# Moving DVE work, the heads' planes and the keys' step in a two-layer graph kernel, with unread products at both ends

## The chip, the cores and the metric

The kernel runs on one core of a Trainium2 chip. The metric is the device time in microseconds (us) of one execution. The engines are PE (TensorE, products), DVE (VectorE), ACT (ScalarE), POOL (GpSimd) and SP (SyncE), which here only issues transfers.

## The reference

64 graphs of 256 nodes with 512 features each go through two layers. Each layer normalizes and clips its input, and adds an attention over the graph's edges to it. Shapes: x (64, 256, 512), float32; adj (64, 256, 256), boolean. In layer 0, `adj` is a mask of what is left out; in layer 1 it is a mask of what is kept.

```python
# layer 0: 8 heads of 64
h = maximum(layernorm(x), 0)
m = h @ map_w.T + map_b                                  # split into heads: sem
n = sem / maximum(norm(sem), 1e-8)
cos_adj = ((n @ n.T) * ~mask > 0.1)                      # cosines over a threshold
q, k = m @ q_w.T + q_b, m @ k_w.T + k_b
p = softmax(where(mask, -1e10, q @ k.T / 8)) * keep      # keep: row's first mask entry is not set
a = cos_adj * p
s = h @ gcn_map_w.T + gcn_map_b
x = x + relu((a @ s) @ gcn_W.T / (a.sum(-1) + 1))
# layer 1: 4 heads of 64
h = maximum(layernorm(x), 0)
q, k, v = h @ Wq, h @ Wk, h @ Wv
attn = softmax(where(mask, q @ k.T / 8, -big))
x = x + (attn @ v) @ Wo + bo
```

## The kernel before

The kernel is a pipeline over the graphs. The function `period(i)` holds the work of four graphs at once: `g` (graph i) finishes its layer 0, `nx` (i+1) goes through its projections, `b` (i-1) finishes its layer 1, and `n2` (i+2) is normalized. `closing()` does the last graph. The order on each engine is the order of the program. PSUM is a ring of eight banks. A projection is done with seven products of blocks instead of eight (`seven_products`), written as a generator: each `next(...)` issues some products on PE, then the additions that read them on DVE.

The parts that the change touches (cuts are marked with `# ...`; a line number such as L546 in a profile is that of the whole file):

```python
def seven_products(left, wt, bias, dst, name, tokens_first=False):
    # ... step 1: products "24" (u2, u4 on ACT)
    pz = bank(f"{name}_z", shape)                         # step 2
    product("z", pz, 0, a11)
    out(0, 0, pz, p2)                                     # DVE, e.g. kT <- p_k_z, u2p_k
    p53 = bank(...); product("53", p53[:, 0], 3, s1); product("53", p53[:, 1], 2, s4)
    p5 = biased(p53[:, 0], 1, 5)                          # u5 on ACT
    yield
    product("z", pz, 4, s2)                               # step 3
    nc.vector.tensor_add(u4, pz, p5)                      # DVE: uup
    out(0, 1, p53[:, 1], u4)
    yield
    product("z", pz, 5, s3)                               # step 4
    out(1, 1, pz, p5); out(1, 0, pz, p4)
    yield

def heads_sent(g, n, av):      # per half n, two planes of 16 bits: ACT copies, SP issues a transpose (DMA)
    for k in range(2):
        nc.scalar.copy(flat.rearrange(...), bits[:, k])
        nc.sync.dma_start_transpose(out=g.heads[...], in_=flat)

def heads_joined(g, n):        # ACT copies the two transposed planes of half n into g.sem
    for k in range(2):
        nc.scalar.copy(bits[:, k, c], g.heads[:, k, c])

def total(g, sm):              # ACT copies the sums of the rows out of PSUM (homes)
    nc.scalar.activation(g.sms, sm, AF.Copy, accum_out=chk[:, g.i, 0:1])

def sums_back(g):              # PE turns the sums (rt), DVE inverts them (r) and applies keep (rk)
    # ...

def heads_added(g, t):         # L542 ff.
    o = sb2.tile([P, H0, DH], F32, tag="xn", name=f"o{g.i}_{t}")
    nc.vector.scalar_tensor_tensor(o, g.sem[:, t, :]..., 0.0, g.rk[:, t, :, None]..., op0=ALU.max, op1=ALU.mult)
    nc.gpsimd.tensor_add(g.xs[:, t, :], g.xs[:, t, :], o...)

def edges(g, home=None):       # POOL makes the edges of a later graph, SP transposes them (mask)
    # ...

def divided(b):                # L646: layer 1's outputs by the sums of their rows
    nc.vector.tensor_mul(b.avs1, b.avs1, b.z)

def result(b, t):              # L651: output product p_o, then DVE adds it to xs
    # ...

def period(i):
    # ... scores, masks, projections m, s, q of nx, cosines of g
    for n in range(2):
        heads_sent(g, n, values(g, n))
    if b:
        nc.scalar.copy(b.avs1, values1(b))
    next(q)                                               # step 4 of q: p_q_z
    total(g, sums(g, lambda c: [g.d[c]], "sm"))
    for n in range(2):
        heads_joined(g, n)
    k = keys(nx)
    next(k)                                               # step 1
    if b:
        nc.scalar.activation(b.rz, b.rz, AF.Copy, accum_out=chk[:, b.i, 3:4])
    sums_back(g)
    heads_added(g, 0)
    # ...
    next(k)                                               # step 2
    heads_added(g, 1)
    if n2:
        edges(n2, g.homes)
    if b:
        divided(b)
    moments(g, f"1_{i}")                                  # DVE: st, mv, rs
    next(k)                                               # step 3
    deviations(g)                                         # ACT: root of rs; DVE: its reciprocal
    normalized(g, f"1_{i}")                               # DVE: xn, twice
    # ...
    if b:
        for t in range(NT):
            result(b, t)                                  # PE: p_o
    # ...
    g.h1T = turned(g, f"1_{i}", "wide")                   # PE: p_t <- xn; ACT: hT
    # ...
    next(k)                                               # step 4, then layer 1's projections of g
```

In the last graph's `closing()` the cosines of two of four pairs of heads stand ahead of the sums `se`, and the other two behind them; the copy of the sums `z` on ACT (`spent`, only for a check of ranges at the end) stands ahead of the reciprocals that read `z` on DVE.

Of the kernel before, what the change touches and what calls it, by code (L numbers as in the profile page):

```python
# [150 lines left out]
def fast_path(ctx, tc, a, w, chk, out):  # L151
# [4 lines left out]
    nc = tc.nc  # L156
# [49 lines left out]
    def normalized(g, tag):  # L206
        g.xn = []
        for t in range(NT):
            xn = sb2.tile([P, D], F32, tag="xn", name=f"xn{tag}_{t}")
            nc.vector.tensor_scalar(xn, g.xs[:, t, :], g.mv[:, t, 0:1], g.rs[:, t:t + 1],  # L210
                                    op0=ALU.subtract, op1=ALU.mult)
            g.xn.append(xn)
# [289 lines left out]
    def heads_joined(g, n):  # L502

        bits = g.sem.bitcast(U16).rearrange("p t (c f k) -> p k c t f", k=2, f=P)
        c = slice(2 * n, 2 * n + 2)
        for k in range(2):
            nc.scalar.copy(bits[:, k, c], g.heads[:, k, c])  # L507

    def sums(g, parts, name):

        sm = bank(f"{name}{g.i}", [P, S])
        for c in range(NKC):
            ps = parts(c)
            for j, part in enumerate(ps):
                for s in range(2):
                    n, k = divmod(2 * c + s, 4)
                    nc.tensor.matmul(sm[32 * k:32 * (k + 1), :], w.two[:, n, :], part[:, s, :],
                                     start=(n == 0 and j == 0), stop=(n == 1 and j == len(ps) - 1))
        return sm

    def total(g, sm):
        g.homes = both_homes(g.i)
        g.sms = g.homes[:, 0, :]
        nc.scalar.activation(g.sms, sm, AF.Copy, accum_out=chk[:, g.i, 0:1])
# [17 lines left out]
    def heads_added(g, t):  # L542
        o = sb2.tile([P, H0, DH], F32, tag="xn", name=f"o{g.i}_{t}")
        nc.vector.scalar_tensor_tensor(o, g.sem[:, t, :].rearrange("p (h d) -> p h d", d=DH), 0.0,  # L544
                                       g.rk[:, t, :, None].to_broadcast([P, H0, DH]), op0=ALU.max, op1=ALU.mult)
        nc.gpsimd.tensor_add(g.xs[:, t, :], g.xs[:, t, :], o.rearrange("p h d -> p (h d)"))  # L546

    def heads_back(g):
        for t in range(NT):
# [61 lines left out]
    def values1(b):  # L611
        av = bank(f"av1_{b.i}")
        for c in range(NIC):
            weighed(av, c, b.v, b.e1[c], 2 * c)
        return av
# [29 lines left out]
    def divided(b):  # L645
        nc.vector.tensor_mul(b.avs1, b.avs1, b.z)  # L646
# [7 lines left out]
    def period(i):  # L654
        g, nx = graphs[i], graphs[i + 1]
        b, n2 = graphs.get(i - 1), graphs.get(i + 2)

        def off_edges(*cs):
            for c in cs:
                masked(g.e[c], g.mask, edges=False)  # L660

        def halved_sums(*cs):
            for c in cs:
                g.d[c] = halves(g.e[c], f"0_{i}_{c}")


        if b:
            b.e1 = [exps(products(b.k1T, b.q1T, c, f"sc1_{b.i}_{c}"), f"1_{b.i}_{c}") for c in range(NIC)]
        for c in range(NKC):
            g.e[c] = exps(products(g.kT, g.qT, c, f"sc0_{i}_{c}"), f"0_{i}_{c}")  # L670
        if b:
            for c in range(NIC):
                masked(b.e1[c], b.mask, edges=True)
        m, s = mapped(nx), messages(nx)
        next(m)
        next(s)
        if n2:
            nc.scalar.activation(n2.rs, n2.rs, AF.Sqrt)

        off_edges(0, 1)  # L680
        halved_sums(1, 0)
        if b:
            b.d1 = [halves(b.e1[c], f"1_{b.i}_{c}") for c in range(NIC)]
        units(g)
        next(m)
        off_edges(2)
        if n2:
            nc.vector.reciprocal(n2.rs, n2.rs)
        halved_sums(2)
        next(m)  # L690
        next(s)
        next(m)

        for c in range(NKC):
            far_off(g, c, cosines(g, c))
            if c == 0:
                off_edges(3)
                halved(nx, lambda: halved_sums(3))
        for c in range(NKC):
            far_added(g, c, 0)  # L700
        squares(nx)
        if n2:
            shifts(n2, f"0_{n2.i}")
            scaled(n2, f"0_{n2.i}", 0)
        q = queries(nx)
        next(q)
        if n2:
            sent(n2, 0)
            scaled(n2, f"0_{n2.i}", 1)
        if b:  # L710
            sums1(b, lambda c: [b.d1[c]])
            own(b, "qk1")
            inverted(b)
        p_n = norms(nx)
        next(s)
        if n2:
            sent(n2, 1)
        if b:
            spread_inverses(b)
            summed_up(b)  # L720
        next(q)
        lengths(nx, p_n)
        for c in range(2):
            far_back(g, c)
            far_added(g, c, 1)
        next(s)
        next(q)
        for c in range(2, NKC):
            far_back(g, c)
            far_added(g, c, 1)  # L730
        next(s)

        g.avs = sb1.tile([P, NKC, S], F32, tag="wide", name=f"avs{i}")
        for n in range(2):
            heads_sent(g, n, values(g, n))
        if b:
            nc.scalar.copy(b.avs1, values1(b))
        next(q)
        total(g, sums(g, lambda c: [g.d[c]], "sm"))
        for n in range(2):  # L740
            heads_joined(g, n)
        k = keys(nx)
        next(k)
        if b:
            nc.scalar.activation(b.rz, b.rz, AF.Copy, accum_out=chk[:, b.i, 3:4])
        sums_back(g)
        heads_added(g, 0)
        if n2:
            joined(n2, f"0_{n2.i}")
            join(n2, 0)  # L750
        next(k)
        heads_added(g, 1)
        if n2:
            edges(n2, g.homes)
        if b:
            divided(b)
        moments(g, f"1_{i}")
        next(k)
        deviations(g)
        normalized(g, f"1_{i}")  # L760
        if i == 0:
            w.finish_seven(w.wqk1)
            w.finish_seven(w.wv1)
        nc.scalar.activation(nx.rn, nx.rn, AF.Sqrt)

        nc.scalar.activation(spare[:, 1:], spare[:, :1], AF.Exp)
        if b:
            for t in range(NT):
                result(b, t)
            nc.sync.dma_start(out=out_t[b.i], in_=b.xs)  # L770
        if i + 3 < B:
            graphs[i + 3] = load(i + 3)
        g.h1T = turned(g, f"1_{i}", "wide")
        if n2:
            join(n2, 1)
        j = queries_keys1(g)
        for t in range(NT):
            nc.gpsimd.tensor_add(g.xs[:, t, :], g.xs[:, t, :], w.bo_b)
        next(k)
        next(j)  # L780
        v = values_in(g)
        next(v)
        nc.vector.reciprocal(nx.rn, nx.rn)
        spread(nx)
        for step in (j, v, j, v, j, v):
            next(step)
        if n2:
            n2.left_h = left_factors(n2.hT, "sh", n2.i)
        if i + 3 < B:
            moments(graphs[i + 3], f"0_{i + 3}")  # L790
            below_zero(graphs[i + 3])

    def closing():
# [3 lines left out]
        for c in range(NKC):  # L797
            g.e[c] = exps(products(g.kT, g.qT, c, f"sc0_{g.i}_{c}"), f"0_{g.i}_{c}")
        units(g)
        co = [cosines(g, c) for c in range(2)]  # L800
        for c in range(NKC):
            masked(g.e[c], g.mask, edges=False)
        se = sums(g, lambda c: both(g.e[c]), "se")
        for c in range(2):
            far_off(g, c, co[c])
        first = sb1.tile([P, S], F32, tag="rn", name="first")
        nc.scalar.activation(first, se, AF.Copy, accum_out=chk[:, g.i, 0:1])
        for c in range(2, NKC):
            far_off(g, c, cosines(g, c))
        if b:  # L810
            b.e1 = [exps(products(b.k1T, b.q1T, c, f"sc1_{b.i}_{c}"), f"1_{b.i}_{c}") for c in range(NIC)]
        for c in range(NKC):
# [23 lines left out]
        if b:  # L836
            nc.scalar.copy(b.avs1, av)
        normalized(g, f"1_{g.i}")
        nc.scalar.activation(spare[:, 1:], spare[:, :1], AF.Exp)
        if b:  # L840
            inverted(b)
# [18 lines left out]
        for c in range(NIC):  # L860
            for j, part in enumerate(both(g.e1[c])):
                for s in range(2):
                    nc.tensor.matmul(z[s * DH:(s + 1) * DH, c, :], w.ones, part[:, s, :], start=(j == 0),
                                     stop=(j == NT - 1))
        spent = sb2.tile([P, NIC, S], F32, tag="xn", name="spent")
        nc.scalar.activation(spent, z, AF.Copy, accum_out=chk[:, g.i, 2:3])
        av = values1(g)
        own(g, "qT")
        for t in range(NT):
            q = slice(t * P, (t + 1) * P)  # L870
            nc.vector.reciprocal(g.z[:, :, q], z[:, :, q])
            nc.vector.tensor_mul(g.avs1[:, :, q], av[:, :, q], g.z[:, :, q])
        nc.scalar.activation(spent, g.z, AF.Copy, accum_out=chk[:, g.i, 3:4])
        if b:
            result(b, 1)
# [5 lines left out]
    def normal_input(g):  # L881
        g.hT = turned(g, f"0_{g.i}", "hT")
        g.left_h = left_factors(g.hT, "sh", g.i)

    with tc.manual_schedule():
        spare = small.tile([P, 2], F32, tag="spare", name="spare", bufs=1)
# [14 lines left out]
            normalized(graphs[n], f"0_{n}")  # L901

        g = graphs[0]
        normal(0)
        normal_input(g)
        edges(g)
# [346 lines left out]
```

## Time and profile before

| | |
|---|---|
| time, median of 3 (range) | 3678.06 us (3676.8 to 3678.59) |
| span of the profiled execution | 3673.2 us |
| PE, DVE, ACT, POOL busy | 98%, 73%, 59%, 61% |
| mean granted clock of PE | 0.998 |

The profile's page gives the busy time of each engine, the costliest groups of instructions, and the chain of work that ended last. A group's line has the source line, the engine, the operation, what it writes and reads, how often, its busy time and mean length, and behind the second bar the idle time of its engine just before it with what ended it. The list of waits names who waited for whom, in us in total, times, and the longest. The timeline has the instructions in order, merged where they repeat. Idle time of an engine counts only where PE, or the end of the program, waits for it in turn.

### The profile page before, as it was taken

What the parts mean: (1) busy time and instruction counts of PE and PEld (TensorE: products, weight loads), DVE (VectorE), ACT (ScalarE), POOL (GpSimd) and SP (SyncE); (2) the same over time, 40 slices, a digit from 0 to 9 for tenths busy, and PEclk for the clock granted to TensorE, in tenths of its full rate; (3) what the DMA queues carried; (4) which work ended last, traced back from release to release, by engine and by line L of the source; (5) the groups of instructions that cost most, each with busy time, mean ns of one, the idle gap of its engine ahead of it and who ended that gap; (6) DMA issues with size and microseconds to landing.
All of it is one profiled execution on the core that took longest, in us unless ns stands there. A gap on an engine that the chain in (4) does not pass through costs nothing.

```text
span 3673.2 us, 78457 instructions
## 1 busy us (share of the span) xinstructions
PE 3590.6 (98%) x29441; PEld 3082.7 (84%) x29441; DVE 2677.3 (73%) x5549; ACT 2164.6 (59%) x5174; POOL 2234.5 (61%) x2044
## 2 busy tenths in 40 slices
PE   8999999999999999999999999999999999999998
PEld 7888888888888888888888888888888888888886
DVE  7767767777677776776777767767777677777776
ACT  4556556666565656665666556555666565656553
POOL 4656666566566665665656656666566566665662
PEclk9999999999999999999999999999999999999999
DMA  4222222222222222222222222222222222222221
GB/s 123 52 67 55 59 67 57 62 57 62 69 55 57 63 61 63 55 60 69 55 60 59 61 67 55 59 67 57 61 57 62 69 55 58 63 59 65 55 54 39
DMA packets 496296, 224.68 MB, mean 61 GB/s; under 512 B 407436, under 2 KB 462248, under 8 KB 495912
## 3 DMA queue, kind: packets, MB, share of 16 engines
q1 hardware_dynamic: 495176, 219.03, 23.6%
q8 instruction: 236, 3.87, 0.5%
q14 instruction: 148, 1.21, 0.1%
q10 hardware_dynamic: 544, 0.52, 0.0%
q0 software_dynamic: 192, 0.04, 0.0%
HBM read 94.41 MB, written 34.34 MB: 35 GB/s over the span
## 4 chain that ended last, share of the span: by engine, by line
PE 86%; DVE 5%; ACT 4%; DMA 2%; issue 2%; POOL 0%; DVEq 0%; SPq 0%; POOLq 0%
PE sc L420 9%; PE av L447 9%; PE p_q L286 7%; PE p_m L286 6%; PE p_o L651 6%; PE p_qk L286 6%; PE p_s L281 6%; PE co L457 5%; PE p_s_z L281 5%; PE p_qk_z L286 5%; PE p_m_z L286 5%; PE p_q_z L286 5%; PE p_v L575 3%; ACT sem L507 3%; DVE o L544 3%; PE p_v_z L575 2%
## 5 line engine op out<-in xcount | busy, mean ns | idle before, releaser
L440 POOL TENSOR_TENSOR d<-e 128x512 f32<-128x512 f32 x376 | 586.4, 1585 | 299.0 <-DVE e L436 296.6
L476 POOL TENSOR_TENSOR d<-d,e 128x512 f32<-128x512 f32 x504 | 651.5, 1325 | 27.9 <-DVE e L481 27.9
L546 POOL TENSOR_TENSOR xs<-xs,o 128x512 f32<-128x512 f32 x126 | 183.7, 1458 | 529.1 <-DVE o L544 529.1
L427 ACT ACTIVATE e<-sc 128x512 f32<-128x512 f32 x768 | 383.3, 648 | 61.2 <-PE sc L420 61.2
L263 POOL TENSOR_TENSOR sh<-hT 128x256 f32<-128x256 f32 x128 | 94.1, 735 | 503.1 <-ACT hT L220 251.1
L436 DVE TENSOR_TENSOR e<-e,mask 128x1024 f32<-128x1024 f32 x256 | 365.3, 1447 | 0.5 <-ACT e L427 0.5
L470 DVE SCALAR_TENSOR_TENSOR e<-co,e 128x256 f32<-128x256 f32 (+1 forms) x1024 | 282.1, 345 | 35.8 <-ACT up L467 35.8
L499 ACT COPY avs<-av 128x512 uint16<-128x512 uint16 x252 | 135.3, 589 | 285.8 <-PE av L447 285.8
L651 PE MATMUL p_o<-wo,own 128*128 128x512 f32 x512 | 235.3, 602 | 50.0 <-DVE own L646 48.9
L467 ACT ACTIVATE up<-co,below 128x128 bf16<-128x128 f32 x512 | 160.3, 365 | 183.1 <-PE co L457 177.7
L447 PE MATMUL av<-e,sem 128*64 128x256 f32 x2048 | 235.6, 382 | 0.3 <-DVE e L481 0.3
L420 PE MATMUL sc<-qT,kT 64*128 64x256 f32 x2048 | 233.7, 376 | 0.0
L311 DVE TENSOR_TENSOR qT<-p_q_z,u5p_q 128x256 f32<-128x256 f32 x64 | 27.2, 425 | 279.6 <-PE p_q_z L286 279.6
L420 PEld LDWEIGHTS sc<-qT,kT 64*128 64x128 f32 x2048 | 220.6, 187 | 1.1 <-ACT hT L220 0.3
L651 PEld LDWEIGHTS p_o<-wo,own 128*128 128x128 f32 x512 | 91.9, 189 | 152.8 <-issue 108.8
L447 PEld LDWEIGHTS av<-e,sem 128*64 128x64 f32 x2048 | 141.2, 137 | 86.8 <-issue 20.9
L481 DVE SCALAR_TENSOR_TENSOR e<-far,e 128x256 f32<-128x256 bf16 x256 | 202.7, 830 | 1.6 <-DMA far<-up 1.5
L197 DVE BATCH_NORM_STATS2 st<-xs 128x6 f32<-128x512 f32 x256 | 173.9, 679 | 26.2 <-POOL xs L546 21.7
L457 PE MATMUL co<-nT 64*128 64x256 f32 (+1 forms) x2048 | 185.0, 330 | 0.0
L457 PEld LDWEIGHTS co<-nT 64*128 64x128 f32 x2048 | 161.3, 187 | 19.5 <-issue 0.4
L507 ACT COPY sem<-heads 128x512 uint16<-128x512 uint16 x252 | 169.5, 761 | 9.0 <-DMA heads<-avs 8.6
L251 ACT COPY hT<-turn 128x1024 uint16<-128x1024 uint16 x124 | 168.4, 1358 | 0.0
(249 smaller groups left out, 9537.6 us busy)
## 6 DMA issues: line engine op xcount, KB each, us to landing
xs<-in_x_dram SPq DMA_DIRECT2D x64, 512.0 KB
nT<-by_rn SPq DMA_DIRECT2D x128, 256.0 KB
out_dram<-xs SPq DMA_DIRECT2D x63, 512.0 KB
own<-by_rz SPq DMA_DIRECT2D x126, 128.0 KB
ad<-in_adj_dram SPq DMA_DIRECT2D x64, 64.0 KB
far<-up SPq DMA_TRANSPOSE x256
heads<-avs SPq DMA_TRANSPOSE x252
turn<-flat SPq DMA_TRANSPOSE x248
```

The source lines that it names most:

```text
L281: nc.tensor.matmul(region, src[:, c, :], wt[:, block, c, :], start=p not in opened, stop=True, skip_group_check=True)
L286: nc.tensor.matmul(region[:, f, :], wt[:, block, c, f * P:(f + 1) * P], src[:, c, :], start=p not in opened, stop=True, skip_group_check=True)
L420: nc.tensor.matmul(ps[s][:, j, :], rows[h, c, j * P:(j + 1) * P], cols[h, c, :], start=True, stop=True)
L427: nc.scalar.activation(e[:, s, :], p.rearrange("p j q -> p (j q)"), AF.Exp, scale=SCALE)
L436: nc.vector.tensor_mul(e, e, m)
L440: nc.gpsimd.tensor_add(d, e[:, :, :S], e[:, :, S:])
L447: nc.tensor.matmul(av[s * DH:(s + 1) * DH, n, :], vs[:, j, (h0 + s) * DH:(h0 + s + 1) * DH], q[:, s, j * S:(j + 1) * S], start=(j == 0), s ...
L457: nc.tensor.matmul(ps[s][:, j, j * P:], g.nT[h, c, j * P:(j + 1) * P], g.nT[h, c, j * P:], start=(j == 0), stop=True, skip_group_check=True)
L470: nc.vector.scalar_tensor_tensor(e, p.rearrange("p j q -> p (j q)")[:, lo:hi], THRESHOLD, e, op0=ALU.is_gt, op1=ALU.mult)
L476: nc.gpsimd.tensor_add(g.d[c], g.d[c], g.e[c][:, :, half * S:(half + 1) * S])
L507: nc.scalar.copy(bits[:, k, c], g.heads[:, k, c])
L651: nc.tensor.matmul(p, b.avs1[:, c, t * P:(t + 1) * P], w.wo1[:, c, :], start=(c == 0), stop=(c == NIC - 1))
```

## The change

In a period: the division of layer 1's outputs goes from behind `heads_added` to right behind the last step of q; the sums of rows go ahead of that step; the first half of the heads' planes is copied before the sums, the second half after; the two additions of `heads_added` go from POOL to DVE; the third step of the keys goes behind the normalization; the range check of `rz` goes a few places later. They are meant to let PE's output product and its turning of xn start without waiting for DVE.

At the ends: `kept_busy` issues products that nothing reads, to keep PE's clock up (14 before the first graph, 9 in the closing); the third pair of cosines in the closing goes ahead of the sums; the copy `spent` goes behind the reciprocals.

```diff
@@ sums split into sums and summed (same products, same order)
@@ heads_added
-        nc.gpsimd.tensor_add(g.xs[:, t, :], g.xs[:, t, :], o.rearrange("p h d -> p (h d)"))
+        nc.vector.tensor_add(g.xs[:, t, :], g.xs[:, t, :], o.rearrange("p h d -> p (h d)"))
@@ period
             nc.scalar.copy(b.avs1, values1(b))
+        heads_joined(g, 0)
+        total(g, sums(g, lambda c: [g.d[c]], "sm"))
         next(q)
-        total(g, sums(g, lambda c: [g.d[c]], "sm"))
-        for n in range(2):
-            heads_joined(g, n)
+        if b:
+            divided(b)
+        heads_joined(g, 1)
         k = keys(nx)
         next(k)
-        if b:
-            nc.scalar.activation(b.rz, b.rz, AF.Copy, accum_out=chk[:, b.i, 3:4])
         sums_back(g)
         heads_added(g, 0)
+        if b:
+            nc.scalar.activation(b.rz, b.rz, AF.Copy, accum_out=chk[:, b.i, 3:4])
 ...
         heads_added(g, 1)
         if n2:
             edges(n2, g.homes)
-        if b:
-            divided(b)
         moments(g, f"1_{i}")
-        next(k)
         deviations(g)
         normalized(g, f"1_{i}")
+        next(k)
@@ closing
-        co = [cosines(g, c) for c in range(2)]
+        co = [cosines(g, c) for c in range(3)]
 ...
-        for c in range(2):
+        for c in range(3):
             far_off(g, c, co[c])
 ...
-        for c in range(2, NKC):
-            far_off(g, c, cosines(g, c))
+        far_off(g, 3, cosines(g, 3))
 ...
         normalized(g, f"1_{g.i}")
+        kept_busy(9, "warm1")
 ...
-        spent = sb2.tile([P, NIC, S], F32, tag="xn", name="spent")
-        nc.scalar.activation(spent, z, AF.Copy, accum_out=chk[:, g.i, 2:3])
         av = values1(g)
 ...
+        spent = sb2.tile([P, NIC, S], F32, tag="xn", name="spent")
+        nc.scalar.activation(spent, z, AF.Copy, accum_out=chk[:, g.i, 2:3])
         nc.scalar.activation(spent, g.z, AF.Copy, accum_out=chk[:, g.i, 3:4])
@@ start
+    def kept_busy(n, name):
+        p = bank(name, [P, P])
+        for _ in range(n):
+            nc.tensor.matmul(p, w.ident, w.ident, start=True, stop=True)
 ...
         g = graphs[0]
+        kept_busy(14, "warm0")
         normal(0)
```

More of the change, by code (lines that the diff above doesn't have):

```diff
@@ L511, in sums, with summed @@
         sm = bank(f"{name}{g.i}", [P, S])
-        for c in range(NKC):
+        summed(sm, parts, range(NKC))
+        return sm
+    def summed(sm, parts, cs):
+        for c in cs:
             ps = parts(c)
@@ L518, in sums @@
                                      start=(n == 0 and j == 0), stop=(n == 1 and j == len(ps) - 1))
-        return sm
     def total(g, sm):
@@ L737, in period @@
             nc.scalar.copy(b.avs1, values1(b))
+        heads_joined(g, 0)
+        total(g, sums(g, lambda c: [g.d[c]], "sm"))
         next(q)
-        total(g, sums(g, lambda c: [g.d[c]], "sm"))
-        for n in range(2):
-            heads_joined(g, n)
+        if b:
+            divided(b)
+        heads_joined(g, 1)
         k = keys(nx)
         next(k)
+        sums_back(g)
+        heads_added(g, 0)
         if b:
             nc.scalar.activation(b.rz, b.rz, AF.Copy, accum_out=chk[:, b.i, 3:4])
-        sums_back(g)
-        heads_added(g, 0)
         if n2:
```

## The prediction

> **What bounds the kernel now.** I read the busy shares first, then the list of waits restricted to PE, then the timeline of one period, then the chain of waits of a longer one. The first lines say that PE has next to nothing left to lose, and where the little is:
>
> ```profile
> PE 3590.6 (98%) x29441; PEld 3082.7 (84%) x29441; DVE 2677.3 (73%) x5549; ACT 2164.6 (59%) x5174; POOL 2234.5 (61%) x2044
> ...
> L546 POOL TENSOR_TENSOR xs<-xs,o 128x512 f32<-128x512 f32 x126 | 183.7, 1458 | 529.1 <-DVE o L544 529.1
> ...
> PE p_o L651 <- DVE own L646: 48.9, 61, 1.1
> ```
>
> PE is busy 3590.6 of 3673.2 us, so all its idle time is 82.6 us, some 14 us of it before its first and after its last product. One wait repeats every period: the output product p_o waits for the division `own` (61 times, 48.9 us, at most 1.1 us). A period (start of one group of scores to the next, read off the 64 repeats of the scores in the chain) is 56.50 us in 35 of the 62 full periods; the other 27 are longer, by 13.2 us together. The 62 take 3516.1 us. The timeline of the typical period that runs from 213.4 to 269.9 us (columns: start, length, engine, line, operation; idle time before it in brackets):
>
> ```profile
> 250.18 0.38 PE L533 MATMUL rt<-ident,homes 128*128 128x128 f32 x2
> ...
> 250.89 0.36 DVE L540 TENSOR_SCALAR rk<-r,keep 128x8 f32<-128x8 f32 x2
> ...
> 251.46 0.69 DVE L544 SCALAR_TENSOR_TENSOR o<-sem,rk 128x512 f32<-128x512 f32 x1 [0.20 <-ACT sem L507]
> ...
> 252.07 0.42 DVE L311 TENSOR_TENSOR kT<-p_k_z,u2p_k 128x256 f32<-128x256 f32 x1
> 252.23 1.27 POOL L546 TENSOR_TENSOR xs<-xs,o 128x512 f32<-128x512 f32 x1 [7.61 <-DVE o L544]
> ...
> 252.40 1.65 DVE L544 SCALAR_TENSOR_TENSOR o<-sem,rk 128x512 f32<-128x512 f32 x1
> ...
> 253.08 1.06 PE L286 MATMUL p_k_z<-sm,wk 128*128 128x128 f32 x8
> 253.97 0.68 DVE L646 TENSOR_TENSOR own<-own 128x512 f32<-128x512 f32 x1
> ...
> 254.13 1.65 POOL L546 TENSOR_TENSOR xs<-xs,o 128x512 f32<-128x512 f32 x1 [0.63 <-DVE o L544]
> 254.57 0.68 DVE L197 BATCH_NORM_STATS2 st<-xs 128x6 f32<-128x512 f32 x1
> 254.80 3.67 PE L651 MATMUL p_o<-wo,own 128*128 128x512 f32 x8 [0.66 <-DVE own L646]
> ...
> 255.81 0.69 DVE L197 BATCH_NORM_STATS2 st<-xs 128x6 f32<-128x512 f32 x1 [0.34 <-POOL xs L546]
> ...
> 256.76 0.17 DVE L200 TENSOR_SCALAR rs<-mv 128x2 f32<-128x2 f32 x1
> ...
> 257.83 1.01 DVE L210 TENSOR_SCALAR xn<-xs,mv,rs 128x512 f32<-128x512 f32 x2
> ...
> 258.52 1.09 PE L219 MATMUL p_t<-ident,xn 128*128 128x128 f32 x8
> ```
>
> The reader should see three things. The second o takes 1.65 us where the first takes 0.69, and it ends 0.55 us after the POOL addition beside it. The division stands behind it, and p_o behind the division. And p_t starts 0.13 us after the first xn (257.83+0.56=258.39) ends, so it too is held by DVE.
>
> How late is PE? The products of p_k_z start (1.06-0.275)/7=0.112 us apart (a product is 275 ns), so p_o was due at 253.08+8x0.112=253.98 and came at 254.80: 0.82 late. Those of p_o start (3.67-0.59)/7=0.44 apart, so p_t was due at 254.80+3.52=258.32 and came at 258.52: 0.20 late. A typical period thus holds 1.02 us that better order could give; 62 of them 63 us, and with the 13.2 us of the longer ones 76 us, 2.1%. That is the ceiling inside the periods.
>
> **What the Trainium skill says.** "SBUF — State Buffer", section "SBUF: two separate sides": VectorE and GpSimd share a port pair under an exclusive lock, which an operation with two SBUF inputs takes against a GpSimd operation that reads SBUF; the loser blocks until the other ends. The 1.65 beside the 1.27 agrees. "GPSIMD Engine Reference", section "3.1 Elementwise — side-by-side cycle accounting": an addition of two tensors is 1.96 times slower on GpSimd at 2048 elements; here 1.27 against 0.68 for a two-input 128x512 on DVE (`own`), 1.87. "TensorE: Matmul & The Clock Gate", section "Part 1: The HAM clock gate": the clock halves after an idle window of about 3.4 us and comes back after about as much work. Here p_t near the end takes 1.94 us for 8 after an idle 2.48, against 1.09 warm, and the clock averages 0.83 from 80 to 100 us after PE's idle 4.44: less idle time was enough.
>
> **The change part by part.**
>
> *Division.* It moves from behind the second o to right behind the p_q_z additions, where DVE has stood idle (4.47 us before those additions, 2.44 before the reciprocal of rt). With the sums now ahead of p_q_z, those additions end about 1.07 us later, near 249.2; the division then ends near 249.9, and rt comes at 250.18. Its inputs (the copy of av at 33.48 us into the period, z loaded by 31) are there. Cost on the path: 0. p_o no longer waits for it.
>
> *Additions.* Two POOL additions of 1.27 (one stretched to 1.65) become two of 0.68 on DVE. DVE's chain in the new order, with starts spaced as in the lines above, from o at 251.29 (rk ends at 251.25; the four copies of the heads' planes now end about 0.75 earlier, since two of them precede the sums' copy): addition +0.74 = 252.03, kT +0.61 = 252.64, o +0.33 = 252.97, addition +0.74 = 253.71, st +0.61 = 254.32, mv +0.72, st +0.10, mv +0.73, rs +0.22 = 256.09, the root on ACT +0.20, its reciprocal +0.24, xn +0.19 = 256.72, end 257.28, so p_t may start at 257.41 instead of 258.52. POOL's port is free then, so no 1.65.
>
> *The keys' step after the normalization.* It takes uup and kT out from between rs and its reciprocal, which were 0.88 us apart (256.76 to 257.64) and need 0.44 for ACT's root alone: 0.44 of the chain's gain is theirs. Their p_k_z is used after p_t, at 258.4; uup ends near 258.05, so nothing new waits.
>
> *What PE then does.* kT ends at 253.06, so the third p_k_z starts at 253.11 (+0.03). p_o follows at 254.01, p_t is due at 254.01+3.52=257.53 and ready at 257.41. It came at 258.52: gain 0.99, less 0.02 where my spacings are coarse: 0.97 x 62 = 60 us.
>
> *The longer periods.* Their transposes of the heads land up to 1.3 us later than a typical period can hide (the last landing 36.3 us into a typical period, up to 38.35 in the longest); in nearly all of these a 16 KB packet of the instruction queue (236 of them in the page's queue list) runs among the transposes. The chain of such a period, 1517.7 to 1574.8:
>
> ```profile
> 1551.61 3.95 DMA heads<-avs
> ...
> 1555.59 0.78 ACT sem L507
> ...
> 1557.00 0.41 DVE kT L311
> ```
>
> Here the new order is worse: kT now stands behind o and the first addition, and p_k_z waits for kT. I rebuilt each of the 62 periods from its landings with the spacings above: the 27 longer ones pay 0.2 to 1.3 us at p_k_z. The sum over all 62 is -57 us, so 3 us are given back.
>
> *The closing's third cosines, ahead of the sums.* The last transposes of far leave about 1.4 us earlier; PE then has the next scores (0.8 earlier) and the av products without the 0.28 wait and the stretched first group: about -1.1 us.
>
> *Unread products.* Nine at the end fill most of the 2.48 idle: p_t is warm, but its reader on ACT is held by a table load until 3641.7 anyway; what is left is p_qk at 1.95 instead of 2.77: -0.8. Fourteen at the start (28 passes, 0.24 each cold) end about when p_t is due at 8.25; the path there is the load of wq (lands at 15.26) and the DVE differences behind it: 0. *The spent copy later*: DVE's reciprocal starts 0.75 earlier, but p_o behind it is then limited by PE: 0. The first period, without a division, gains about 0.5 from the shorter chain.
>
> Sum: -57-0.5-1.1-0.8 = -59 us, 3619. I take 3621, because p_t and its second half each have only 0.12 us of slack in my rebuild.
>
> **The rivals.** (1) The DVE chain takes over as the bound: 0.12 us of slack is less than my spacings are sure of; each 0.1 us beyond it costs 6 us, so a chain 0.4 longer would give 3638. For it: p_t is held by DVE already. Against: the 1.65 and the POOL wait before st go for certain. (2) The transposes' landing becomes the bound more often, since kT waits for the additions: if half the periods lost 0.8, 3632. For it: the 27 long periods. Against: the copies on ACT are 0.75 earlier, so only landings later than 37.05 count. (3) Masks leave about 7 us earlier (POOL is free) and share the DMA engines with the heads' last transposes: a landing delayed by 0.6 in each period would give 3640. Against: they are issued behind them. (4) All of it hidden, long periods too: 3598.
>
> **Range and chances.** 3621, 8 in 10 between 3606 and 3639. Faster by over 2% needs under 3604.5, nearly the whole ceiling: 0.06. Slower by over 2% would need a new wait of over 2 us a period, which no line suggests: 0.01. Within 2%: 0.93.
>
> **What would show it.** Right: the wait of p_o on `own` gone, o at 0.69 both times, typical periods near 55.5, p_k_z waiting for kT a few tenths in periods with late heads, half-speed clock gone near 3640. Wrong: p_t waiting for xn in most periods (rival 1), ACT's copies of heads waiting in most (2, 3), or typical periods near 56.

## The result, and the profile after

| | before | changed |
|---|---|---|
| median (range) | 3677.43 us (3673.48 to 3678.59) | 3595.49 us (3594.11 to 3597.51) |
| ratio, 95% interval | | 0.9779 (0.9763 to 0.9796) |
| span of the profiled execution | 3673.2 us | 3595.7 us |
| start to second group of scores | 99.66 us | 101.05 us |
| typical period, x 62 | 56.50, 3503.0 us | 55.11, 3416.8 us |
| what the longer periods add to 62 typical ones | 13.1 us | 22.5 us |
| from the last period's end to the end | 57.42 us | 55.36 us |

The kernel is 2.2% faster: 82 us by the medians, 77.5 us between the two profiles, where I had predicted 56. The page of the changed kernel, first its busy times, then p_o's group (behind the second bar the idle time before it):

```profile
PE 3560.4 (99%) x29487; PEld 3057.2 (85%) x29487; DVE 2703.4 (75%) x5675; ACT 2169.1 (60%) x5174; POOL 2050.1 (57%) x1918
...
L654 PE MATMUL p_o<-wo,own 128*128 128x512 f32 x512 | 230.5, 593 | 0.0
```

The wait of p_o is gone altogether. PE's busy time also fell, by 30 us, although 46 products were added: something became cheaper on PE itself. The list of PE's waits over the full periods has one of size left:

```profile
PE p_k_z L286 <- DVE kT L311: 14.7, 21, 1.2
```

These 21 waits are in the longer periods. Before, this wait came to 1.4 us in 4 of them. The same stretch of the same period as in the prediction, which now runs from 212.8 to 267.9 us (start, length, engine, line, operation):

```profile
245.55 1.07 PE L521 MATMUL sm<-d,two 128*32 128x256 f32 x16
...
246.55 1.16 PE L286 MATMUL p_q_z<-sm,wq 128*128 128x128 f32 x8
...
247.55 1.95 PE L286 MATMUL p_k<-mT,wk 128*128 128x128 f32 x16
...
248.42 0.68 DVE L649 TENSOR_TENSOR own<-own 128x512 f32<-128x512 f32 x1
...
249.33 0.38 PE L536 MATMUL rt<-ident,homes 128*128 128x128 f32 x2
...
250.38 0.69 DVE L547 SCALAR_TENSOR_TENSOR o<-sem,rk 128x512 f32<-128x512 f32 x1
...
251.11 0.69 DVE L549 TENSOR_TENSOR xs<-xs,o 128x512 f32<-128x512 f32 x1
251.72 0.42 DVE L311 TENSOR_TENSOR kT<-p_k_z,u2p_k 128x256 f32<-128x256 f32 x1
252.05 0.68 DVE L547 SCALAR_TENSOR_TENSOR o<-sem,rk 128x512 f32<-128x512 f32 x1
252.23 1.12 PE L286 MATMUL p_k_z<-sm,wk 128*128 128x128 f32 x8
252.77 0.69 DVE L549 TENSOR_TENSOR xs<-xs,o 128x512 f32<-128x512 f32 x1
253.19 3.60 PE L654 MATMUL p_o<-wo,own 128*128 128x512 f32 x8
...
255.75 1.00 DVE L210 TENSOR_SCALAR xn<-xs,mv,rs 128x512 f32<-128x512 f32 x2
256.62 1.04 PE L219 MATMUL p_t<-ident,xn 128*128 128x128 f32 x8
```

The division stands in DVE's idle time, 0.68 us and off the path. From o to xn DVE takes 255.75-250.38=5.37 us, so p_t could start at 255.75+0.55+0.13=256.43 and starts at 256.62. That is 0.19 of slack: p_t no longer waits. What DVE still costs a typical period is 0.06 at the third p_k_z, which comes just behind kT (1.12 long here, 1.06 elsewhere). Set side by side, start to start, only six of PE's groups differ from before in a typical period:

| group (to the next one's start) | before | changed |
|---|---|---|
| p_q_z, last step of q | 1.088 | 0.995 |
| p_k, first step | 1.889 | 1.786 |
| p_k_z, third step, to p_o | 1.719 | 0.953 |
| p_o to p_t | 3.723 | 3.436 |
| p_t | 0.923 | 0.873 |
| last p_v to the scores | 0.653 | 0.564 |

These sum to 1.39 us. The third to fifth rows, 1.10, are the waits that I meant. The other 0.29 I had not in the sum at all. The sums and their neighbours in the kernel before (timeline of PE):

```profile
246.20 1.16 PE L286 MATMUL p_q_z<-sm,wq 128*128 128x128 f32 x8
247.29 1.07 PE L517 MATMUL sm<-d,two 128*32 128x256 f32 x16
248.29 2.05 PE L286 MATMUL p_k<-mT,wk 128*128 128x128 f32 x16
```

p_k has 16 products in both, and took 2.05 us here against 1.95 above, with no wait named in either. p_q_z is 1.16 long in both, but here the sums start 1.09 after it, and above p_k starts 1.00 after it. `128*32` says that the sums' weights are 32 columns wide; the products of q and k are 128 wide.

### The profile page after: what moved, and what is told of

The parts are those of the page before. It is cut to its first block, busy times and chain, and to the rows that moved or that the text cites. A ratio compares the mean times of both kernels' runs of the same rounds, so it can differ in the third digit from the quotient of the medians.

```text
span 3595.7 us, 78427 instructions
## 1 busy us (share of the span) xinstructions
PE 3560.4 (99%) x29487; PEld 3057.2 (85%) x29487; DVE 2703.4 (75%) x5675; ACT 2169.1 (60%) x5174; POOL 2050.1 (57%) x1918
## 4 chain that ended last, share of the span: by engine, by line
PE 93%; DMA 3%; DVE 1%; ACT 1%; issue 1%; SPq 0%; POOL 0%; DVEq 0%; POOLq 0%; ACTq 0%
PE sc L420 10%; PE av L447 8%; PE p_m L286 7%; PE p_q L286 7%; PE p_qk L286 6%; PE p_o L654 6%; PE p_s L281 6%; PE co L457 5%; PE p_qk_z L286 5%; PE p_m_z L286 5%; PE p_s_z L281 5%; PE p_k_z L286 5%; PE p_k L286 4%; PE p_q_z L286 4%; PE p_v L578 3%; PE p_v_z L578 2%
## 5 line engine op out<-in xcount | busy, mean ns | idle before, releaser
L507 ACT COPY sem<-heads 128x512 uint16<-128x512 uint16 x252 | 185.4, 767 | 69.2 <-DMA heads<-avs 67.9
L420 PEld LDWEIGHTS sc<-qT,kT 64*128 64x128 f32 x2048 | 198.5, 187 | 22.7 <-ACT hT L220 0.3
L781 POOL TENSOR_TENSOR xs<-xs,bo_b 128x512 f32<-128x512 f32 x126 | 157.8, 1274 | 0.0
```

Of the source, the lines that this page charges most:

```text
L420: nc.tensor.matmul(ps[s][:, j, :], rows[h, c, j * P:(j + 1) * P], cols[h, c, :], start=True, stop=True)
```

## The experiments

Each starts from the changed kernel unless said otherwise. "Typical" is the median of the 62 periods in its profile. For the changed kernel it stands for 55.11, the length of 29 of its 62 and the median when it ran again; the median of its first profile is 55.14. The ratio is against the kernel before on the same chip.

**Sums behind.** What is the unexplained 0.2 us?

```diff
         heads_joined(g, 0)
-        total(g, sums(g, lambda c: [g.d[c]], "sm"))
         next(q)
         if b:
             divided(b)
+        total(g, sums(g, lambda c: [g.d[c]], "sm"))
```

> The changed kernel with only the sums of rows put back behind the last step of q on PE (everything else as changed). Theory A, that PE pays for each switch between narrow (32-column) weights and full ones, and that the sums' new place next to the av products saves one pair of switches: the group p_q_z takes 1.09 instead of 1.00 us and the following p_k 1.89 instead of 1.79, the typical period goes from 55.11 to 55.31, the time from 3595 to about 3607. Rival B, that the PE gain of 0.2 us is slack of some other engine: typical period stays 55.11, time 3595.

Measured: 3604.58 us, ratio 0.9811 (0.9794 to 0.9827), typical 55.32. p_q_z went back to 1.088 and p_k to 1.888, and nothing else moved. A holds, B falls: the gain is PE's own, and lies at the borders, where one group of products ends and the next begins. Not only 32 columns do this: in the kernel before, a group also goes on 0.09 longer where 64 columns follow (p_s_z in front of av, 0.96 against 0.87) or 64 rows (p_m_z in front of the cosines, 0.98 against 0.89). Where only the moving side changes, from 128 to 256 columns, it costs nothing (p_m_z in front of p_s, 0.89). So the shape of the weights matters here, not the length of the products.

**Sums split.** The same cost doubled, with the same number of products.

```diff
-        total(g, sums(g, lambda c: [g.d[c]], "sm"))
+        sm = bank(f"sm{i}", [P, S])
+        summed(sm, lambda c: [g.d[c]], (0, 1))
         next(q)
+        summed(sm, lambda c: [g.d[c]], (2, 3))
+        total(g, sm)
```

> The changed kernel with the sums cut in two: half of them in front of the last step of q, half behind it. This adds two borders between narrow and full weights to the one that the changed kernel has there, with the same products. Theory A, that PE pays about 0.1 us at each border: typical period 0.2 above 55.11, the same as with all sums behind (55.31), time about 3605 to 3607. Rival B, that the sums' place matters through the products' number or through ACT's copy: typical period 55.1 to 55.15.

Measured: 3605.40 us, ratio 0.9815 (0.9800 to 0.9830), typical 55.44, 0.33 above. The timeline of PE in a period of it:

```profile
1912.72 0.64 PE L521 MATMUL sm<-d,two 128*32 128x256 f32 x8
1913.29 1.16 PE L286 MATMUL p_q_z<-sm,wq 128*128 128x128 f32 x8
1914.38 0.64 PE L521 MATMUL sm<-d,two 128*32 128x256 f32 x8
1914.95 2.05 PE L286 MATMUL p_k<-mT,wk 128*128 128x128 f32 x16
```

p_q_z and p_k pay the 0.09 and 0.10 again (1.09 from start to start; 2.05 long), and the two half sums take 0.57 each where the whole took 1.00. A holds, with 0.14 more in the period than it said, which is what the sums cost more as two groups than as one.

**Narrow groups together**, on top of the trial version below: zb goes behind the cosines, p_n ahead of the av products.

```diff
         squares(nx)
+        if b:
+            sums1(b, lambda c: [b.d1[c]])
 ...
-            sums1(b, lambda c: [b.d1[c]])
 ...
-        p_n = norms(nx)
 ...
-        lengths(nx, p_n)
 ...
+        p_n = norms(nx)
         g.avs = ...
 ...
             nc.scalar.copy(b.avs1, values1(b))
+        lengths(nx, p_n)
```

> The trial version before with two more groups of narrow weights moved next to others: zb behind the cosines, p_n in front of the av products. Theory A, that each pair of switches between narrow and full weights costs PE 0.2 us: typical period 0.1 to 0.3 below 55.11, time 6 to 18 us below that of the trial version it builds on. Rival B, that the 0.2 us of the sums' move was special to its place: typical period 55.1, no difference.

Measured: 3608.86 us, ratio 0.9822 (0.9806 to 0.9839), typical 55.49, 26 us slower than the version it builds on. Start to start, p_q fell by 0.09 and p_s_z by 0.10, but zb rose by 0.11 and p_n by 0.02: 0.06 less in all. I had miscounted the borders. There are four as before, since zb now stands between the cosines and p_q, and p_n between p_s_z and av. And PE now comes earlier to a product that DVE holds (its list of waits):

```profile
PE p_s_z L281 <- DVE uup_s L331: 14.2, 62, 0.5
```

With this wait p_s_z starts 0.39 later, and its restart takes 0.10 more, so the period grew by 0.44 over the trial version's 55.05. A's price of 0.1 at a border stands, its forecast does not.

**Division alone**, on the kernel before: `divided(b)` goes from in front of `moments` to behind `next(q)`, nothing else.

> The kernel before with only the division moved to behind the last step of q. Theory A, that the division on DVE alone held p_o, and xn then holds p_t: the wait of p_o is gone, the DVE chain ends 0.6 us earlier, p_t waits about 0.4 us, typical period near 55.9 instead of 56.50, time about 3640. Rival B, that the wait only moves from p_o to p_t: period 56.4 or more, time over 3670. Rival C, that the division alone gives all that the DVE moves give: typical period 55.4, time about 3610.

Measured: 3646.82 us, ratio 0.9926 (0.9909 to 0.9942), typical 56.13. A, less 0.2: p_o's wait is gone and p_t waits 0.58 us in the median period.

**Division back**, the reverse: `divided(b)` behind `heads_added(g, 1)` again.

> The changed kernel with only the division back behind the second addition on DVE. Theory A: p_o starts at 41.4 instead of 40.4 us into the period, typical period 56.1 to 56.2, time 3655 to 3662. Rival B, that the additions on DVE and the keys' new place had already made room for it: typical period 55.3 or less, time under 3610.

Measured: 3662.57 us, ratio 0.9967 (0.9956 to 0.9979), typical 56.21: A, at its upper edge. Its list of PE's waits shows the old wait with nearly the old total:

```profile
PE p_o L654 <- DVE own L649: 52.5, 61, 0.9
```

Without the division's move, all the others together give 11 of the 82 us.

**Additions back on POOL.**

```diff
-        nc.vector.tensor_add(g.xs[:, t, :], ...)
+        nc.gpsimd.tensor_add(g.xs[:, t, :], ...)
```

> The changed kernel with the two additions of heads_added back on POOL. Theory A, that the additions' move is a main part of the gain (as my prediction's chain had it): p_t waits 0.5 us or more for xn in a typical period, period 55.6 or more, time 3625 or more. Theory B, that the division's and the keys' new places do it all, because POOL's 1.27 can overlap with kT on DVE: xn at most 0.2 us later than now, inside PE's slack of 0.19, typical period 55.1 to 55.2, and kT ahead of the late heads' additions takes some tenths off the longer periods: time 3588 to 3600.

Measured: 3602.32 us, ratio 0.9804 (0.9788 to 0.9820), typical 55.28. Nearer to B, but 2 us outside it. A period's timeline (it starts at 2489.64):

```profile
2527.25 0.69 DVE L547 SCALAR_TENSOR_TENSOR o<-sem,rk 128x512 f32<-128x512 f32 x1
...
2527.86 0.42 DVE L311 TENSOR_TENSOR kT<-p_k_z,u2p_k 128x256 f32<-128x256 f32 x1
...
2528.02 1.28 POOL L549 TENSOR_TENSOR xs<-xs,o 128x512 f32<-128x512 f32 x1 [7.17 <-DVE o L547]
2528.19 1.66 DVE L547 SCALAR_TENSOR_TENSOR o<-sem,rk 128x512 f32<-128x512 f32 x1
...
2531.23 0.70 DVE L197 BATCH_NORM_STATS2 st<-xs 128x6 f32<-128x512 f32 x1 [0.56 <-POOL xs L549]
...
2532.82 1.00 DVE L210 TENSOR_SCALAR xn<-xs,mv,rs 128x512 f32<-128x512 f32 x2
2533.51 1.08 PE L219 MATMUL p_t<-ident,xn 128*128 128x128 f32 x8
```

The lock is back (1.66 beside 1.28), and still xn starts 43.18 us into the period, against 42.98 with the additions on DVE: POOL's first addition ran beside kT and the second o, and only its second one holds DVE (0.56 before the second st). So p_o to p_t takes 0.08 and p_t 0.05 more, the third p_k_z 0.06 less, as kT no longer stands behind an addition on DVE, and 0.09 more goes at the scores. The latter has no engine's work behind it that the profile shows: with the additions on POOL, before and here, the first scores product carries waits for both DVE and PE, with them on DVE only for DVE. That goes together in all the runs here (0.65 in the four with POOL, 0.56 in the ten with DVE); that the second wait is the cause is not shown.

**Keys' step back** in front of `deviations`.

> The changed kernel with only the third step of the keys back in front of the root and the normalization. Theory A, that its two additions on DVE lengthen the chain to xn by 0.44 us, of which PE's slack of 0.19 hides a part, and that a restart of PE after a wait costs up to 0.1 more: p_t waits, typical period 55.4 to 55.5, time 3612 to 3618. Rival B, that ACT's root hides them: 55.1, 3595.

Measured: 3611.93 us, ratio 0.9831 (0.9815 to 0.9848), typical 55.41: A. p_t starts 0.25 later, and pays 0.05 more once started.

**Sums alone**, on the kernel before: `total(...)` goes ahead of `next(q)`.

> The kernel before with only the sums in front of the last step of q. Theory A, that in the kernel before PE's 0.2 us are not what counts, because p_o waits for DVE: the copies of the heads on ACT and the rows' sums come earlier, o starts up to 0.43 earlier, and the period falls by that, to about 56.1, time about 3652. Rival B, that PE's 0.2 us come through alone: 56.3, about 3662. Rival C, that nothing comes through: 56.5, 3674.

Measured: 3658.21 us, ratio 0.9957 (0.9942 to 0.9972), typical 56.18, and 56.07 or 56.08 in 28 of the 62 periods. A in the typical period; the time is 6 us above what it named, with more and longer periods over it. Here the sums work through DVE's earlier start, not through PE's borders: o and the division start 0.38 us earlier in the period, p_o still waits for the division 61 times, and so starts 0.37 earlier.

**No unread products**: both calls of `kept_busy` out.

> The changed kernel without any unread products. Theory A, that the 14 at the start backfire (PE warms early, cools again while it waits for the differences of wm, and POOL's factors start earlier and block those differences on the shared port): the first scores start at about 44.4 instead of 45.2 us, and the end grows by about 0.8 us, so that the total stays within 1 us of 3595. Rival B, that the 14 at the start help: the first scores start later than 45.2. Side question: if the extra bank that they take in the ring is what took a wait off the first scores of a period, the typical period goes from 55.11 to 55.20 and the time to about 3601.

Measured: 3595.05 us, ratio 0.9783 (0.9767 to 0.9799), typical 55.11 with every group as in the changed kernel. The first scores start at 44.27 instead of 45.17, and the end takes 57.30 instead of 55.36 us: A at the start, and twice its loss at the end. In all there is no difference: the unread products gained nothing. The mean clock (before the DMA share and rate at the line's end) in one stretch of the start, first in the changed kernel, then in "sums behind", which has the 14 products too:

```profile
12.60:16.10 3.50, 3.10 (x14) 3.14 (x15) 2.10 (x4) 1.02 (x4) 2.48 (x4) 0.51 1.10 350
```

```profile
12.60:16.10 3.50, 3.21 (x29) 3.24 (x30) 2.07 (x4) 1.94 (x7) 2.37 (x4) 1.00 1.10 347
```

The 14 products warm the clock early, and PE then idles 2.33 us for the differences of wm. In the changed kernel the clock halves after that; in "sums behind", after 2.13 us idle, it doesn't, and the first scores start at 44.07. The section "Part 1: The HAM clock gate" of the Trainium skill's "TensorE: Matmul & The Clock Gate" has the clock judged in windows that run on by themselves; that one idle stretch costs the clock in one program and a like one does not in another agrees with it. The other runs say the same: of the seven profiles with the 14 products, four have a half-speed stretch there and first scores at 45.17 to 45.74, three have none and first scores at 44.03 to 44.25. Two of them, one of each kind, idled 1.91 us ("division back" and "keys' step back"). Without the 14, six of seven have first scores at 44.03 to 44.41, and one at 45.21, where the clock rose 4 us later than in the others. So the length of the idle time does not decide it, and the 0.9 us are in part chance.

**The longer periods: kT between o and the first addition** (the trial version; it also drops the 14 products, puts 12 into the first period's idle stretch, and makes layer 1's weight differences earlier there).

```diff
-        heads_added(g, 0)
 ...
-        next(k)
+        heads_added(g, 0, lambda: next(k))      # o, then kT, then the addition
         heads_added(g, 1)
```

What it is for shows in a longer period of the changed kernel (1209.4 to 1265.9):

```profile
1247.58 0.77 ACT L507 COPY sem<-heads 128x512 uint16<-128x512 uint16 x1 [2.37 <-DMA heads<-avs]
...
1248.38 0.69 DVE L547 SCALAR_TENSOR_TENSOR o<-sem,rk 128x512 f32<-128x512 f32 x1 [1.34 <-ACT sem L507]
...
1249.72 0.42 DVE L311 TENSOR_TENSOR kT<-p_k_z,u2p_k 128x256 f32<-128x256 f32 x1
...
1250.19 0.60 PE L286 MATMUL p_k_z<-sm,wk 128*128 128x128 f32 x3 [1.16 <-DVE kT L311]
```

The last heads land late, o waits for their copy, kT waits behind o and the addition, and PE behind kT. The last heads land 38.16 us into this period, 36.35 into a usual one. The queue list from 1241 to 1250 us has one packet of the instruction queue among 2471 of the transposes' queue:

```profile
q8 instruction: 1, 0.02, 1.1%
```

> A trial version on top of the changed kernel: the additions of the keys' second step (kT) go between o and the first addition, so that PE's third p_k_z need not wait behind the additions when the heads land late; no unread products at the start, but 12 in the first period's idle stretch; the differences of layer 1's weights earlier in the first period. Theory A, that kT behind the late heads is what the longer periods pay: PE's waits before p_k_z mostly go, but xn is late in those periods as well, so only 0.1 to 0.2 us of each is saved; the sum over the median period falls from 20.9 to 16 to 18 us, the start by 3 us; time 3586 to 3592. Rival B, that the wait of p_k_z is all there is: 1.0 us less in the worst periods, the sum falls to 8, time about 3579.

Measured: 3582.69 us, ratio 0.9752 (0.9736 to 0.9768), typical 55.05. Its PE waits:

```profile
PE p_t L219 <- DVE xn L210: 2.9, 12, 0.3
PE p_k_z L286 <- DVE kT L311: 0.4, 1, 0.4
```

The longer periods add 11.7 us to 62 typical ones instead of 22.5 (20.9 over the median, as A counts), more of a gain than A said and less than B: p_k_z's wait is all but gone, and a smaller one of p_t for xn took its place. Two gains were not expected: 0.06 in the typical period, as p_k_z no longer waits for kT at all (0.953 fell to 0.893), and 4.4 us instead of 3 at the start.

**Both once more on one chip.**

> The changed kernel once more, to stand on one chip beside the trial version: 3592 to 3598, typical period 55.11; the time that the longer periods add (15 to 23 us over the median period so far) is chance, from where the instruction fetches fall.

> The trial version with kT between o and the first addition once more: 3579 to 3585, typical period 55.05, 10 to 14 us below the changed kernel on the same chip, of which some 4 are at the start, 4 in the typical periods and the rest in the longer ones.

Measured: changed 3594.13 us (3590.92 to 3596.21), ratio 0.9781 (0.9767 to 0.9794); trial 3583.44 (3582.03 to 3584.61), ratio 0.9753 (0.9739 to 0.9766). The ranges do not meet: the trial version is 10.7 us faster than the changed kernel. Its longer periods add 15.5 us this time, against 18.9, a gain of 3.4 instead of the 9 to 11 above. How much it gains there is thus not settled, and A is the nearer this time. Between these two profiles the start gives 4.8 us, the typical periods 3.8, and the end 0.6.

## Why the prediction was wrong, point by point

The direction and the wait were right, the size was not: 3595.5 lies below the range, whose lower end was 3606.

- *"That is the ceiling inside the periods"*: this is the step that failed. I measured how late p_o and p_t came and took the rest of PE's sequence as fixed. It is not. Against my 0.97 per typical period stand 1.39: 0.196 at the sums' borders (shown by putting them back and by splitting them), 0.09 at the scores (gone whenever the additions are on DVE), and 1.10 instead of 0.97 for the waits, since a group that starts after a wait also pays for its start: p_o's second product came 0.50 after its first instead of 0.43. The lines for it lay in the profile before: p_k took 2.05 behind the sums and 1.95 elsewhere, and from p_q_z to the sums it was 1.09, where eight such products take 0.89 elsewhere. 0.42 x 62 is 26 us. Against it the longer periods cost 6 and the start 2 us more than I had.
- *Division*: right. It costs nothing on the path in its new place, and it is the key: 28 us alone, 67 us when taken out.
- *Additions*: the chain was right (5.43 us predicted from o to xn, 5.37 measured), its owner was not. On POOL it is 0.20 longer, so their move is worth 7 us, and most of the chain's gain comes from the division and the keys' step that no longer stand in it.
- *Keys' step*: right; 16 us when undone. Its 0.44 comes out as 0.25 later plus 0.05 for the restart, after the 0.19 of slack.
- *Longer periods*: right in kind: p_k_z waits 14.7 us for kT where heads land late, and 1.4 before. I had 3 us for it in all; they add 9.4 more than before in the first profile and 5.8 in the repeat, so the size is in part chance.
- *Start*: wrong, +1.4 instead of -0.5. The 14 products did not end without effect: where the clock halved behind them, the first scores came 0.8 to 1.3 us later than the 44.41 before, and where it did not, 0.2 to 0.4 earlier. The first period took 55.88 instead of 55.24, where I had 0.5 less: p_t waits 3.09 there instead of 4.44, but p_k_z waits 0.96 for kT and p_qk_z 0.81 for qk. With the keys' step back the latter wait is gone, and the period takes 55.45.
- *End*: -1.9 predicted, -2.1 measured, but the agreement is luck. With the third cosines moved, the closing's first scores stand 8.84 us before the next instead of 9.42: 0.58 where I had 1.1. With the nine products the clock never halved near the end, in ten profiles. Without them it did in the kernel before (57.42) and in "no unread products" (57.30), but not in "division alone" and "sums alone", which have the old closing and took 56.34 and 56.47. So about 1 us of the gain hangs on whether the clock happened to halve before. The later `spent` was not tried alone.
- *Rivals*: 1 and 3 did not happen (p_t has slack; 23 of the 62 last landings come after 37.05 us, and 27 did before). 2 happened in the longer periods alone. 4, all hidden at 3598, is nearest, and was still above the result.

From 56.50 x 62 and 13.1 to 55.11 x 62 and 22.5 is -76.8, with +1.4 and -2.1 the 77.5 us of the profiles.

## What to carry to other kernels

When the bound engine is 98% busy, its idle time is not all that an order can give: compare the same group of products in different surroundings, start to start, before you write down a ceiling. Move work off the path into the idle stretch that the waiting engine already has, and ask what each instruction between two dependent ones on an in-order engine is doing there. Where a transfer is sometimes late, put the work that doesn't need it ahead of the work that does.

## What the runs showed that I had not expected

A border between products with 32-column and with 128-column weights cost PE about 0.1 us (0.093 and 0.103 at the two borders that the sums left, 0.093 and 0.102 where they were put back), and it shows as a longer group or a later start of the next, not as a wait. The clock halved after 2.33 us idle at the start in one program and not after 2.13 in another, and after 1.91 us it did in one and did not in another. Fetches of instructions of 16 KB went with late landings of the heads, at most 1.9 us later than the usual 36.35 us into the period: in all 23 periods of the changed kernel whose last landing came after 37.05 us such a fetch began between 29 us and the landing, and in 14 of the other 39. That the fetch delays them is not shown by a run without it.
